# Block sums of A21 and A22, and one transfer of squares, put elsewhere in the written order of a factorization-machine kernel

## The chip, the cores and the metric

The kernel runs on one core of one Trainium2 chip. The metric is device time in microseconds (us); the time of a version is the median of several executions. Besides these, one execution is recorded by the hardware profiler; all lines of profiles in this document are of such an execution. PE is TensorE's matmul row and PEld its weight loads, DVE is VectorE, ACT is ScalarE, POOL is GpSimd, SP is SyncE, and a q behind a name is that engine's sequencer, which issues transfers and waits.

## The reference

Input x has 1024 rows of 512 features. There are 64 embeddings, each a 512 x 512 matrix, one linear layer of 512 x 512 and a bias:

```python
out_lin = x @ lin_w.T + lin_b
xv = jnp.einsum('bf,efm->bem', x, weight)
zp = jnp.einsum('bf,efm->bem', jnp.square(x), jnp.square(weight))
interaction = 0.5 * jnp.sum(jnp.square(xv) - zp, axis=1)
return out_lin + interaction
```

All is float32. The second product is linear in the squared weights, so the kernel sums these over the embeddings first (`w2_sum`) and multiplies by the squares of x once, at the end. What remains is 64 products of x with an embedding, squared and summed.

## The kernel before

**Tiling.** x is taken as 2 x 2 blocks A11, A12, A21, A22 (`"1"`, `"2"`, A21 apart, `"4"`), each again as 2 x 2 quarters. The embeddings are worked through in 16 groups of four ("quads", q = 0 to 15). In a quad the product is done with seven products in place of eight, on two levels: seven units i (in the order 1, 2, 6, 7, 5, 3, 4), each with seven products o (1, 5, 6, 2, 7, 3, 4), for two halves j of the rows. For this, sums and differences of blocks of x (`outer_x`, `inner_x`; made once) and of weights (`outer_t`, `inner_t`; on GpSimd in each quad) are needed. A product ends in a PSUM bank x, v or y; ScalarE copies x to y (line 481), VectorE and ScalarE read the banks and add them to earlier parts of the unit chain in the buffers `z` (lines 450 to 473). Two adds of unit 5 (`rest`, line 478) are GpSimd's. ScalarE squares the finished z in place (line 503), and GpSimd issues transfers that add z to the running sum `acc` (`gather`, line 512).

**Weights.** Four buffers hold a quad's weights (`WB[kk][v]`, 1 MB each), loaded by SP (line 364). ScalarE squares them (`w_squares`, line 521), two instructions to half a quad's pair, into the one buffer `w2_sb` (`w_sb` in the profile). GpSimd issues a transfer that adds this buffer to `w2_sum` (`w_sum` in the profile, line 528). The next squares can be written only when that transfer has landed. The very first squares go straight to `w2_sum`.

**Order.** Each engine works in the order of a list. `Stream.at(t, fn)` enters a piece of work under a time t of an abstract clock, and `run` carries the pieces out sorted by t; so t only decides the order on each engine, and waits between engines do the rest. One quad is 98 of these units, one product two. An engine does not go on past a piece that waits.

**The beginning.** Before quad 0 the linear layer is done. `lin` (line 215) makes the rows of A11's products; then come two units in the same seven-product form, unit 0 for A12 (`lin_unit(0, ...)`, line 347) and unit 1 for A21 and A22 (`lin_unit(1, ...)`, line 348). Products are line 272. VectorE reads a bank of unit 0 in `lin_add` (line 315), at 0.25 behind its product: banks v, y, x, v, y, y, at -20.25, -19.25, -18.25, -17.25, -16.25 and -13.65. Product "4" of unit 0 adds to bank y after the read of "7". Unit 1 needs the sums 5, 6, 7, 3 of the quarters of A21 and A22, which `a21_a22_sums` makes on VectorE (line 252, kk = 0 for A21 and 1 for A22, in the order 5, 5, 6, 6, 7, 7, 3, 3). The list at line 595 gives them their times; where fewer times stand than there are pieces, the rest follow the last one at 0.1 each. In the same list stand the x sums for unit 3, six instructions of GpSimd (`outer_x("3")`, line 174, and `inner_x("3")`, lines 181 to 184).

**GpSimd in the first quad.** Around the piece that moves, its order before is: t6 of unit 7 (line 399, 34.5), the six x sums for unit 3 (36.9 to 37.4), the gather into acc (38.8), t4 of unit 7 (39.7), the transfer into `w2_sum` (42), then tp of unit 5 (43.1).

Of the kernel before, what the change touches and what calls it, by code (L numbers as in the profile page):

```python
# [28 lines left out]
def kernel(  # L29
# [31 lines left out]
    nc = tc.nc  # L61
# [45 lines left out]
    def xsl(i, o):  # L107
        return xs[:, SLOT[i], SLOT[o], :]
# [37 lines left out]
    def quarter(r, kk, n):  # L146

        w = slice(0, 3) if n is None else n
        for i, rk in BLOCK.items():
            if rk == (r, kk):  # L150
                return a21[i] if n == 3 else xs[:, SLOT[i], w, :]
        return A21[:, w, :]

    def outer_x(i, eng=nc.vector):
        if i in BLOCK:
            return []

        def put(n):
            w = slice(0, 3) if n is None else n

            def of(o):
                return a21[o] if n == 3 else xs[:, SLOT[o], w, :]

            def src(r, kk):
                return quarter(r, kk, n)

            if i == "5":
                eng.tensor_add(of(i), src(1, 0), src(1, 1))
            elif i == "6":
                eng.tensor_sub(of(i), of("5"), src(0, 0))  # L170
            elif i == "7":
                eng.tensor_sub(of(i), src(0, 0), src(1, 0))
            else:
                eng.tensor_sub(of(i), src(0, 1), of("6"))

        return [lambda: put(None), lambda: put(3)]

    def inner_x(i, eng=nc.vector, which="5673"):
        add, sub = eng.tensor_add, eng.tensor_sub
        fns = {  # L180
            "5": lambda: add(xsl(i, "5"), a21[i], xsl(i, "4")),
            "6": lambda: sub(xsl(i, "6"), xsl(i, "5"), xsl(i, "1")),
            "7": lambda: sub(xsl(i, "7"), xsl(i, "1"), a21[i]),
            "3": lambda: sub(xsl(i, "3"), xsl(i, "2"), xsl(i, "6")),
        }
        return [fns[o] for o in which]
# [45 lines left out]
    def lin_x(kk, o, r=1):  # L232
        if r == 0:
            return xsl("2", o)
        if kk == 1:
            return xsl("4", o)
        return A21[:, SLOT[o]] if o in "124" else A21_SUMS[:, "5673".index(o)]


    def a21_a22_sums():  # L240
        def put(kk, o):
            def of(o):
                return lin_x(kk, o)

            raw = a21["4"] if kk else A21[:, 3]
            fn, a, b = {
                "5": lambda: (nc.vector.tensor_add, raw, of("4")),
                "6": lambda: (nc.vector.tensor_sub, of("5"), of("1")),
                "7": lambda: (nc.vector.tensor_sub, of("1"), raw),
                "3": lambda: (nc.vector.tensor_sub, of("2"), of("6")),  # L250
            }[o]()
            fn(of(o), a, b)

        return [
            lambda o=o, kk=kk: put(kk, o)
            for o in "5673"
            for kk in range(2)
        ]
# [257 lines left out]
    def w_squares(t, q, v, u):  # L516
        first = q == v == u == 0

        def sq(kk):
            o = (w2_sum if first else w2_sb)[:, ts(kk, 2)]  # L520
            nc.scalar.activation(o, WB[kk][v][:, u], AF.Square)  # L521

        for kk in range(2):
            st.at(t + 0.1 * kk, lambda kk=kk: sq(kk))
        if not first:
            st.at(
                t + (3.2 if t < 0 else 5),
                lambda: nc.gpsimd.dma_start(w2_sum, w2_sb, accum_op=ALU.add),
            )

# [10 lines left out]
    for q in range(NQ):  # L541
# [29 lines left out]
        for k, n, r, times in (  # L571
# [5 lines left out]
            for j in range(2):  # L577
                t = g0 + 14 * k + 7 * j + 14.6
# [8 lines left out]
        for n, t in enumerate(w_times):  # L587
            w_squares(g0 + t, q, n // 2, n % 2)
# [6 lines left out]
    for sums, *times in (  # L595
        (inner_x("1"), -29),
        (inner_x("2"), -22),
        (a21_a22_sums(), -21, -19, -18, -16.9, -15.9),
        (outer_x("5") + outer_x("6") + inner_x("6"), -13.5),
        (outer_x("7"), -6),  # L600
        (inner_x("7", which="75"), -5.4),
        (inner_x("7", nc.gpsimd, "6"), -5),
        (inner_x("7", nc.gpsimd, "3"), -4.7),
        (inner_x("5", nc.gpsimd), 27.2),
        (outer_x("3", nc.gpsimd) + inner_x("3", nc.gpsimd), 36.9),
    ):
        for n, fn in enumerate(sums):
            k = min(n, len(times) - 1)
            st.at(times[k] + 0.1 * (n - k), fn)
# [233 lines left out]
```

## Time and profile before

| | us |
|---|---|
| median of 3 runs | 1411.3 (1410.71 to 1411.66) |
| profiled execution | 1412.15 |
| its span, first to last instruction | 1410.3 |
| PE busy | 1402.1 |
| DVE busy | 867.2 |
| ACT busy | 621.3 |
| POOL busy | 1252.2 |
| mean rate of the DMA engines | 194 GB/s |

A row of a timeline gives the start, the duration, the engine, the line and operation, what is written and read, the shape and the count; in brackets, the engine's idle time before it and what ended that. In the chain of waits the columns are start, duration and what the time went to; "issue" is time in which the engine waited for nothing that the profile shows. A transfer that GpSimd or SP issues shows as a short instruction; the data move later.

### The profile page before, as it was taken

How to read it: one execution, taken by the hardware profiler on the slowest of the kernel's cores; microseconds unless marked ns; L12 is line 12 of the kernel's file. 1: busy time of each engine (PE TensorE's matmuls, PEld its weight loads, DVE VectorE, ACT ScalarE, POOL GpSimd, SP SyncE). 2: the span in 40 equal slices, each digit the busy share in tenths (PEclk: the TensorE clock that was granted, in tenths of full speed). 3: DMA queues.
4: the chain of work that ended last, by engine and by line, in shares of the span. 5: the costliest groups of instructions: out<-in, count | busy, mean ns of one | idle time of the engine just before them, and what ended most of it. 6: DMA issues, size and time to landing. Idle time of an engine off the chain costs nothing.

```text
span 1410.3 us, 11201 instructions
## 1 busy us (share of the span) xinstructions
PE 1402.1 (99%) x3352; PEld 637.6 (45%) x3352; DVE 867.2 (61%) x1270; ACT 621.3 (44%) x826; POOL 1252.2 (89%) x815
## 2 busy tenths in 40 slices
PE   9999999999999999999999999999999999999999
PEld 6444444444444444444444444444444444444446
DVE  6555666656566565666656566565656656566565
ACT  2435353443534434353443534444353453435443
POOL 3999899998999989899898988989898898989984
PEclk9999999999999999999999999999999999999999
DMA  5199898898989899898999989989898999989975
GB/s 216 30 222 212 179 221 178 206 212 205 193 170 233 179 212 210 190 212 168 218 196 220 197 171 228 182 201 214 193 206 173 223 187 218 203 175 225 181 165 134
DMA packets 58108, 273.63 MB, mean 194 GB/s; under 512 B 5440, under 2 KB 8000, under 8 KB 41792
## 3 DMA queue, kind: packets, MB, share of 16 engines
q0 software_dynamic: 36432, 198.20, 71.7%
q1 hardware_dynamic: 21328, 74.19, 15.1%
q10 hardware_dynamic: 288, 0.52, 0.1%
q8 instruction: 27, 0.44, 0.1%
q14 instruction: 33, 0.27, 0.1%
HBM read 72.61 MB, written 2.10 MB: 53 GB/s over the span
## 4 chain that ended last, share of the span: by engine, by line
PE 92%; POOL 4%; DMA 2%; issue 1%; DVE 0%; ACT 0%; POOLq 0%; ACTq 0%; DVEq 0%
PE y L427 39%; PE v L427 26%; PE x L427 26%; DMA acc<-z 1%; DMA w_sum<-w_sb 1%; POOL tp L397 1%; PE lin L215 1%; POOL t L386 0%; POOL t L401 0%; PE y_lin L272 0%; POOL t L399 0%; POOL acc L512 0%; POOL z L478 0%; POOL w L386 0%; DMA t<-lin_wT 0%
## 5 line engine op out<-in xcount | busy, mean ns | idle before, releaser
L427 PE MATMUL y<-t,xs 128*128 128x512 f32 x896 | 421.3, 592 | 0.0
L481 ACT COPY y<-x 128x512 f32<-128x512 f32 x224 | 127.7, 570 | 607.5 <-PE x L427 607.4
L473 DVE TENSOR_TENSOR z<-y,s 128x512 f32<-128x512 f32 x192 | 132.9, 692 | 249.5 <-PE y L427 249.5
L427 PEld LDWEIGHTS y<-t,xs 128*128 128x128 f32 x896 | 170.2, 190 | 214.3 <-issue 212.1
L503 ACT ACTIVATE z<-z 128x1024 f32<-128x1024 f32 x256 | 260.1, 1054 | 11.7 <-POOL z L478 9.2
L427 PE MATMUL x<-w,xs 128*128 128x512 f32 x512 | 248.4, 592 | 0.0
L427 PE MATMUL y<-tp,xs 128*128 128x512 f32 x448 | 229.4, 594 | 2.3 <-ACT s L450 2.3
L427 PE MATMUL v<-tp,xs 128*128 128x512 f32 x448 | 229.6, 594 | 0.0
L512 POOL DMA_DIRECT2D acc<-z x190 | 213.2, 1152 | 14.4 <-DMA acc<-z 9.2
L397 POOL TENSOR_TENSOR tp<-w 128x1024 f32<-128x1024 f32 x64 | 175.0, 2734 | 26.6 <-PE y L427 22.0
L427 PE MATMUL x<-t,xs 128*128 128x512 f32 x384 | 188.3, 592 | 0.0
L478 POOL TENSOR_TENSOR z<-z,s 128x1024 f32<-128x1024 f32 x64 | 149.6, 2355 | 41.8 <-DVE s L473 41.8
L473 DVE TENSOR_TENSOR z<-v,s 128x512 f32<-128x512 f32 x192 | 132.9, 692 | 73.4 <-PE v L427 71.6
L464 DVE TENSOR_TENSOR z<-y,z 128x512 f32<-128x512 f32 x192 | 132.5, 690 | 57.2 <-PE y L427 57.2
L386 POOL TENSOR_TENSOR t<-w,t 128x1024 f32<-128x1024 f32 x64 | 164.2, 2727 | 0.0
L464 DVE TENSOR_TENSOR z<-x,z 128x512 f32<-128x512 f32 x192 | 132.3, 689 | 36.5 <-PE x L427 35.0
L427 PEld LDWEIGHTS x<-w,xs 128*128 128x128 f32 x512 | 97.3, 190 | 122.0 <-issue 120.8
L397 POOL TENSOR_TENSOR tp<-t 128x1024 f32<-128x1024 f32 x48 | 130.1, 2711 | 19.4 <-PE y L427 19.2
L427 PEld LDWEIGHTS y<-tp,xs 128*128 128x128 f32 x448 | 85.0, 190 | 109.4 <-issue 106.0
L427 PEld LDWEIGHTS v<-tp,xs 128*128 128x128 f32 x448 | 85.4, 191 | 107.5 <-issue 103.9
L427 PE MATMUL v<-w,xs 128*128 128x512 f32 x256 | 130.7, 592 | 0.0
L521 ACT ACTIVATE w_sb<-w 128x1024 f32<-128x1024 f32 x126 | 125.9, 1050 | 6.3 <-DMA w_sum<-w_sb 4.7
(117 smaller groups left out, 1456.4 us busy)
## 6 DMA issues: line engine op xcount, KB each, us to landing
w<-weight SPq DMA_DIRECT2D x64, 1024.0 KB, 13.1
acc<-z POOLq DMA_DIRECT2D x128, 512.0 KB, 8.3
w_sum<-w_sb POOLq DMA_DIRECT2D x63, 1024.0 KB, 9.5
acc<-z POOLq DMA_DIRECT2D x62, 1024.0 KB, 8.4
w<-x SPq DMA_DIRECT2D x2, 1024.0 KB, 8.0
out<-z SPq DMA_DIRECT2D x7, 256.0 KB, 2.3
xs<-x SPq DMA_DIRECT2D x2, 384.0 KB, 7.4
t<-lin_wT ACTq DMA_DIRECT2D x2, 256.0 KB, 4.3
```

The lines of the kernel that those rows point to most:

```text
L215: nc.tensor.matmul(LIN[n], quarter(0, 0, (0, 1, 3, 2)[2 * s + l])[:, ts(j, P)], lw_sb[:, l, :], start=(l == 0), stop=(l == 1),)
L386: nc.gpsimd.tensor_sub(OUTER[i][:, u], a[:, u], b[:, u])
L397: nc.gpsimd.tensor_sub(t, b[:, 1], b[:, :, 0])
L427: nc.tensor.matmul(d[bank], xsl(i, o)[:, ts(j, P)], operand_b(q, i, o), start=start, stop=True, skip_group_check=True,)
L464: nc.vector.tensor_add(zblk(q, dst, j, b), d[bank], zblk(q, addend, j, b))
L473: nc.vector.tensor_add(s if both else zblk(q, dst, j, b), d[bank], s)
L478: nc.gpsimd.tensor_add(place(q, n)[:, 1, j], place(q, src)[:, 1, j], d["s"])
L481: st.at(t0 + 0.5, lambda: nc.scalar.copy(d["y"], d["x"]))
L503: lambda u=u: nc.scalar.activation(z[:, u, j], z[:, u, j], AF.Square),
L512: nc.gpsimd.dma_start(o, z, accum_op=ALU.add)
L521: nc.scalar.activation(o, WB[kk][v][:, u], AF.Square)
```

## The change

Three numbers of the order change. The sum "5" of A22 goes from -19 to -20.9, so it follows "5" of A21 at once, ahead of the reads of banks v and y at -20.25 and -19.25. The six sums 6, 7 and 3 go to -15.9 and after, so "6" of A21 and of A22, which stood at -18 and -16.9 among the reads, now follow the read of bank y at -16.25. For quad 0, v = 1, u = 0, the transfer of squares into `w2_sum` goes from 5 to 1.5 behind the squares, from 42 to 38.5 in GpSimd's order. The x sums for unit 3 go from 36.9 to 38.9. GpSimd's order becomes: t6 of unit 7, the transfer into `w2_sum`, the gather into acc, the six x sums, t4 of unit 7, tp of unit 5.

```diff
         if not first:
             st.at(
-                t + (3.2 if t < 0 else 5),
+                t + (3.2 if t < 0 else 1.5 if q == 0 and v == 1 and u == 0 else 5),
                 lambda: nc.gpsimd.dma_start(w2_sum, w2_sb, accum_op=ALU.add),
             )
...
-        (a21_a22_sums(), -21, -19, -18, -16.9, -15.9),
+        (a21_a22_sums(), -21, -20.9, -15.9),
...
-        (outer_x("3", nc.gpsimd) + inner_x("3", nc.gpsimd), 36.9),
+        (outer_x("3", nc.gpsimd) + inner_x("3", nc.gpsimd), 38.9),
```

## The prediction

> **What bounds the kernel now.** The page first. TensorE is busy nearly all the time, so what counts is where it isn't, or where it runs slowly.
>
> ```profile
> PE 1402.1 (99%) x3352; PEld 637.6 (45%) x3352; DVE 867.2 (61%) x1270; ACT 621.3 (44%) x826; POOL 1252.2 (89%) x815
> ```
>
> Then the busy time by stretches (stretch, length; busy us of PE, PEld, DVE, ACT, POOL; granted clock; DMA share; GB/s):
>
> ```profile
> 0.00:35.00 35.00, 32.49 (x111) 21.57 (x112) 21.64 (x36) 10.28 (x16) 13.15 (x16) 1.00 0.59 218
> 70.00:92.00 22.00, 19.69 (x43) 8.41 (x42) 10.61 (x16) 5.17 (x8) 20.31 (x15) 0.92 0.89 178
> 92.00:110.00 18.00, 18.00 (x43) 7.96 (x43) 13.41 (x21) 10.10 (x12) 16.94 (x12) 1.00 1.00 264
> 175.00:1345.00 1170.00, 1170.00 (x2728) 517.95 (x2727) 724.17 (x1058) 524.28 (x695) 1066.17 (x686) 1.00 0.91 200
> ```
>
> From 175 to 1345 us TensorE has no gap. It loses time at the start, in 70 to 92 (where alone the clock is under 1.00), and a little at the end. The chain of waits, in order of time, goes through both early places:
>
> ```profile
> 15.67 0.22 DVE xs L252
> 15.89 2.17 issue
> ...
> 73.04 10.88 DMA w_sum<-w_sb
> ...
> 87.02 1.65 PE y L427 x2
> ```
>
> One DVE sum with 2.17 us in it that no wait explains; and a transfer of squares that ScalarE, and behind it TensorE, waits for. Both are what the diff moves. The timeline of the first place, all engines:
>
> ```profile
> 15.51 2.35 POOL L397 TENSOR_TENSOR tp<-w 128x1024 f32<-128x1024 f32 x1 [3.31 <-DMA w<-weight]
> ...
> 15.67 2.47 DVE L252 TENSOR_TENSOR xs<-z,xs 128x256 f32<-128x256 f32 x1
> ...
> 20.76 1.10 PE L272 MATMUL y_lin<-z,xs 128*128 128x256 f32 x4 [1.49 <-DVE acc L315]
> ```
>
> The sum of A22 ("5" of kk=1) at 15.67 meets a GpSimd operation that began 0.16 us before; it lasts 2.47 us where its like takes 0.41, and ends just after GpSimd does. Three bank reads queue behind it on VectorE, and TensorE's last product of unit 0 waits for the third. The second place:
>
> ```profile
> 71.22 0.85 POOL L512 DMA_DIRECT2D acc<-z  x1
> ...
> 73.04 1.17 POOL L528 DMA_DIRECT2D w_sum<-w_sb  x1
> ...
> 84.00 2.00 ACT L521 ACTIVATE w_sb<-w 128x1024 f32<-128x1024 f32 x2 [4.69 <-DMA w_sum<-w_sb]
> ...
> 104.16 2.00 ACT L521 ACTIVATE w_sb<-w 128x1024 f32<-128x1024 f32 x2 [1.58 <-DMA w<-weight]
> ```
>
> The first of the two ScalarE lines is the wait for the transfer; the second, for a load of weights, matters for what is late next.
>
> **What the Trainium skill says.** "SBUF — State Buffer", Who interferes with whom: a VectorE instruction with two SBUF inputs contends with a GpSimd instruction that reads SBUF, the later one blocks until the first ends; one with at most one SBUF input doesn't. The trace agrees: the sum's 2.47 us, against bank reads of 0.69 us under running GpSimd work. "TensorE: Matmul & The Clock Gate", What's actually happening: after an idle window of some 3.4 us, free-running, the array runs at half clock until it has been busy for one. The trace agrees in kind, with only 2.3 us idle: after 87.02 the steps between products are 1.44, 1.71 and 1.22 us instead of 0.86. "DMA: Bandwidth & Descriptors", Issuing engines are not separate DMA queues: SP's and GpSimd's transfers interleave on the same 16 engines. The trace agrees: in 92 to 110 their share is 1.00.
>
> **The change part by part.** The sum is made against the span, 1410.3 us (the profiled execution took 1412.15); the median shown is 1411.3. I take the same difference off each.
>
> *Block sums (VectorE).* Eight sums before, eight after, none added. "5" of kk=1 goes from behind two bank reads to right behind "5" of kk=0. It then starts at 13.42 (0.34 after its neighbour, the pitch of such sums at 20.53, 20.86, 21.20) and ends by 13.83, inside VectorE's wait of 0.63 us before 14.12: cost nothing. If that cover were gone it would cost 0.34. Its new wait is on block A22: the semaphores put its last landing at 12.88, so 0.54 to spare, and 0.29 more until it holds up the read at 14.12. GpSimd is idle from 12.20 to 15.51, so no collision. The other six sums go behind the read at 16.52 + 1.14 = 17.66 (a read follows the start of its products by 1.14: 12.98 to 14.12). They begin at about 18.3, after GpSimd's operation ended (17.86) and before its next (30.31). TensorE needs "6" three products later, at about 21.7; it is ready by 19.1. Six of 0.34 end near 20.4, when the last read of unit 0 is due (20.24): 0.15 us, covered by VectorE's later wait of 1.08 at 28.87.
> TensorE's gain: products before the gap start at 17.38 and 18.24, after it at 20.76, 21.70, 22.56. With 0.86 a step 21.70 would be 19.96: **1.74 us**. GpSimd's restart at 30.31 waits for a VectorE sum that itself follows TensorE, so it moves 1.74 too.
>
> *The transfer of squares (GpSimd).* No operation is added. In GpSimd's order the issue of w_sum (73.04) and of one gather into acc (71.22) come ahead of the six x sums for "3" (65.80 to 71.27, 5.4 us); the product's t4 stays behind them. Each issue takes 0.60 of GpSimd's time (71.22 to 71.82), so the x sums end 1.2 us later, 20 us before their unit at about 94; everything from t4 on keeps its place. The new wait: the squares of that transfer end at 65.09, GpSimd arrives at 65.84, 0.75 to spare. Behind that wait would stand the gather, the x sums and all later GpSimd operands.
> w_sum is now issued at 65.84 - 1.74 = 64.1. The first such transfer, alone, took 8.2 us (48.49 to 56.72 by the semaphores), this one 10.88 behind the gather. It lands between 72.3 and 75.0; ScalarE wants its buffer at 79.31 - 1.74 = 77.6. The 4.69 us wait goes. TensorE gains 87.02 - (82.83 + 2 x 0.86) = 2.47 of idle time, and of the three slow steps 4.37 - 3 x 0.86 = 1.80: **4.27 us**. Both parts together: 6.0.
>
> *Where the stall goes.* GpSimd gains only 1.74 there. The rests at 92.44 waited 1.89 for VectorE; now GpSimd arrives at 88.81, late by 2.4 against TensorE's 6.0. Its tp for "4" ends at 101.9, while TensorE's use of it (107.70) moves to 101.7: 0.2 given back, at most 5.8 left. More comes from the weights of the second quad. SP issues them at 84.82 behind GpSimd's outer "4", so at 83.1. ScalarE already waits for the second load at 104.16 (its last landing is 104.05), then squares (1.91), squares again (0.97) and copies y (0.57): 107.66, and TensorE uses that y at 109.42. So 1.76 to spare: the total gain is at most what the load comes earlier, plus 1.76.
> How much earlier? The DMA engines are full from 72 to 106. The gather issued at 81.54 had to wait for w_sum until 83.92; now it starts when issued, at about 79.8 + 1.4 = 81.2, 2.7 us earlier, and the loads behind it. Against it: the gathers of 97.04 and 103.08 come 3.6 to 4.5 us earlier and share with the load. Bounds: 2.7 if they don't matter, 1.74 (its issue alone) if they do. I take 2.3, as only their lead over the load, one or two us, counts. Gain 2.3 + 1.76 = **4.1** (3.5 to 4.5). Afterwards TensorE has no gap to the end: GpSimd waits for it or for VectorE some 5 us a quad (41.2 and 41.8 us in 16), so it makes up its lag, and the tail's chain starts from TensorE at 1357.6. Forecast 1410.3 - 4.1 = 1406.2 of span, 1407.2 median.
>
> **The rivals.**
> A, likeliest (0.57): as above, gain 3.3 to 4.9.
> B (0.15): the load comes early enough, or ScalarE's copy has more room; only the 0.2 of tp is lost: 5.8, 1405.5. For it: its first engines finish at 100.6, the last alone at 104.05. Against: the same spread in later quads.
> C (0.15): the new gap on TensorE (6.0 - 4.1 = 1.9) trips its clock again and costs up to 1.8 more: gain about 2.3, 1409.0. For it: 2.3 us of idling did so at 87. Against: the gap of 1.49 at 19.27 did not.
> D (0.05): the sum gains nothing, because A22 arrives after 15: second part alone, limited by the load, about 2.5, 1408.8.
> E, slower (0.08): the two gathers, each about 2.5 us of full DMA at 200 GB/s, get wholly ahead of the load's last engines. It lands 5 - 2.7 = 2.3 later than before; with 1.76 to spare 0.5 is lost, and the clock's price of 1.8 to 3 comes on top: 2.3 to 3.5 slower, 1414. It decides from a landing 1.76 us later than today's 104.05. Against it: one of them is already before that landing today.
>
> **How the numbers follow.** A difference under 0.2% (2.8 us) can't be told from none here. A and B are faster, and a fifth of C: 0.75. The rest of C and D: same, 0.17. Slower: 0.08. From B's gain of 5.8 (and a little for the runs' spread) to the weak end of C, 1.3: 1405.4 to 1410.0, which leaves out E and edges.
>
> **What would show it.** After: a sum L252 of about 0.41 at 13.4, no 2.47; no TensorE wait on VectorE near 19; w_sum issued near 64, no ScalarE wait on it; clock 1.00 in 70 to 90. Then a ScalarE wait on weights grown from 1.58 to some 5 us near 97 to 102, and a TensorE gap of 1 to 2 us just before 105. Wrong if TensorE gets no gap there (B), if slow steps follow it (C), or if new gaps come in later quads, where I count none.

## The result and the profile after

The changed kernel takes 1407.41 us (median of 16 runs, 1406.9 to 1408.36), against 1410.82 us (1409.65 to 1411.66) for the kernel before beside it: a ratio of 0.9977, 95% interval 0.997 to 0.9985. That is 0.23% faster, clear of no change, and inside the forecast's range; the forecast was 1407.2. The profiled span is 1406.4 us (forecast 1406.2).

The page of the kernel after, busy time of each engine:

```profile
PE 1401.1 (100%) x3352; PEld 637.8 (45%) x3352; DVE 863.9 (61%) x1270; ACT 621.5 (44%) x826; POOL 1252.6 (89%) x815
```

Its busy time by the same stretches as before (stretch, length; busy us of PE, PEld, DVE, ACT, POOL; granted clock; DMA share; GB/s):

```profile
0.00:35.00 35.00, 34.15 (x114) 22.51 (x115) 20.32 (x36) 11.23 (x17) 14.21 (x16) 1.00 0.58 218
70.00:92.00 22.00, 22.00 (x53) 9.79 (x52) 13.54 (x21) 7.40 (x11) 21.77 (x16) 1.00 0.74 149
92.00:110.00 18.00, 16.76 (x40) 7.01 (x39) 11.83 (x18) 8.66 (x11) 17.18 (x12) 1.00 1.05 276
175.00:1345.00 1170.00, 1170.00 (x2727) 518.40 (x2726) 721.87 (x1057) 526.60 (x697) 1066.37 (x687) 1.00 0.91 199
```

The gap and the slow clock in 70 to 92 are gone. In 92 to 110, where TensorE had no gap before, it now lacks 1.24 us. From 175 to 1345 TensorE has no gap, as before. The chain of waits after, in order of time, passes through the first place without leaving TensorE, and leaves it at a new one:

```profile
18.04 1.73 PE x_lin L272 x8
19.77 0.86 PE y_lin L272 x4
...
84.09 17.82 DMA w<-weight
...
105.59 1.96 PE y L427 x4
```

VectorE's timeline after, at the moved sum:

```profile
13.09 0.41 DVE L252 TENSOR_TENSOR xs<-z,xs 128x256 f32<-128x256 f32 x1
14.62 0.69 DVE L315 SCALAR_TENSOR_TENSOR s_lin<-v_lin,acc 128x512 f32<-128x512 f32 x1 [1.12 <-PE v_lin L272]
```

The sum that took 2.47 us takes 0.41, inside a wait. ScalarE's timeline after, at the new place, and then TensorE's:

```profile
102.01 2.00 ACT L521 ACTIVATE w_sb<-w 128x1024 f32<-128x1024 f32 x2 [4.93 <-DMA w<-weight]
103.92 1.04 ACT L503 ACTIVATE z<-z 128x1024 f32<-128x1024 f32 x1
104.87 0.58 ACT L481 COPY y<-x 128x512 f32<-128x512 f32 x1
```

```profile
102.77 1.13 PE L427 MATMUL v<-tp,xs 128*128 128x512 f32 x2 [0.41 <-POOL tp L397]
103.73 1.02 PE L427 MATMUL v<-w,xs 128*128 128x512 f32 x2
105.59 1.96 PE L427 MATMUL y<-t,xs 128*128 128x512 f32 x4 [0.84 <-ACT y L481]
```

ScalarE waits 4.93 us for quad 1's second load (it landed at 101.91) instead of 1.58. TensorE loses time twice, first for GpSimd's tp of unit 4, then for the copy of y that stands behind ScalarE's squares. Counted in steps of 0.86 us from the product group at 100.49, the one at 107.38 is 1.7 us late.

### The profile page after: what moved, and what is told of

It is laid out like the page before. It is cut to its first block, busy times and chain, and to the rows that moved or that the text cites. A ratio compares the mean times of both kernels' runs of the same rounds, so it can differ in the third digit from the quotient of the medians.

```text
span 1406.4 us, 11202 instructions
## 1 busy us (share of the span) xinstructions
PE 1401.1 (100%) x3352; PEld 637.8 (45%) x3352; DVE 863.9 (61%) x1270; ACT 621.5 (44%) x826; POOL 1252.6 (89%) x815
## 4 chain that ended last, share of the span: by engine, by line
PE 95%; DMA 2%; POOL 2%; issue 0%; ACT 0%; DVE 0%; POOLq 0%; ACTq 0%; DVEq 0%
PE y L427 40%; PE x L427 27%; PE v L427 26%; DMA w<-weight 1%; DMA acc<-z 1%; PE lin L215 1%; PE y_lin L272 1%; PE x_lin L272 0%; PE v_lin L272 0%; POOL z L478 0%; POOL acc L512 0%; DMA t<-lin_wT 0%; POOL w_sb L660 0%; POOL tp L397 0%; POOL w L640 0%
## 5 line engine op out<-in xcount | busy, mean ns | idle before, releaser
L452 DVE TENSOR_TENSOR s<-v,z 128x512 f32<-128x512 f32 x160 | 110.5, 690 | 30.5 <-PE v L427 29.2
```

Of the source, the lines that this page charges most:

```text
L452: nc.vector.tensor_add(o, d[bank], zblk(q, addend, j, b))
```

## Experiments

Medians of the first four runs are against 1411.15 us for the kernel before beside them, of the next three against 1411.08, of the last three against 1410.97.

**The block sums alone.**

```diff
-        (a21_a22_sums(), -21, -19, -18, -16.9, -15.9),
+        (a21_a22_sums(), -21, -20.9, -15.9),
```

> The block sums moved, the transfer and the x sums left as before. My theory (a VectorE sum met a running GpSimd operation and held up three bank reads): the 2.47 us sum becomes 0.41, TensorE's wait on VectorE near 20 us is gone, all later work comes 1.7 us earlier, ScalarE still waits about 4.7 us for the transfer of squares and TensorE runs slowly behind it. Span 1408.6, 1.7 us below before. Rival (what is won early is lost again at the transfer or at the weights of quad 1): span within 0.5 us of before.

Measured 1409.09 us, ratio 0.9988 (0.9982 to 0.9995): 2.1 us faster. In the profile the linear product groups go 18.02, 18.89, 19.75, where before 18.24 was followed by 20.76 and 21.70: 1.73 us, as worked out. The bank reads at 15.63 and 16.50 run under GpSimd's operation (15.12 to 17.49) and take their usual 0.69. ScalarE still waits 4.74 us for the transfer and TensorE 2.36 us behind it. But no slow steps follow that wait here, and the span is 1406.6, 2 us below what I expected; the clock is taken up below.

**The transfer and the x sums alone.**

```diff
-                t + (3.2 if t < 0 else 5),
+                t + (3.2 if t < 0 else 1.5 if q == 0 and v == 1 and u == 0 else 5),
...
-        (outer_x("3", nc.gpsimd) + inner_x("3", nc.gpsimd), 36.9),
+        (outer_x("3", nc.gpsimd) + inner_x("3", nc.gpsimd), 38.9),
```

> The transfer of squares ahead of the x sums, the block sums left as before. My theory: the ScalarE wait on the transfer and the slow TensorE stretch go (4.3 us), but the second weight load of quad 1 is issued when it was, and lands only about 1 us earlier since the DMA engines have less ahead of it; ScalarE then waits some 4 us for it and TensorE gets a gap of about 1.5 us before 109. Gain 1.0 + 1.8 = 2.8, span 1407.5. Rival (the two stalls are independent and the load doesn't limit): gain 4.3, span 1406.0. If the two parts simply add up, this and the sums alone make the whole change's 3.9.

Measured 1408.39 us, ratio 0.9983 (0.9976 to 0.999): 2.8 us faster. ScalarE has no wait on the transfer, waits 4.61 us for the weights from then on, and TensorE waits 0.45 us for tp at 103.36 and 0.47 us for the copy of y at 105.82. The two parts alone give 2.1 and 2.8 us; together they give 3.4. They don't add up. With the transfer alone, quad 1's second load already holds TensorE up. With the sums alone hardly any spare time is left there: ScalarE's copy of y ends at 105.59, and TensorE uses it at 105.82. Both gains also hold a part of the same clock, which is counted below, at the kernel before once more.

**Only the "5" of A22 moved.**

```diff
-        (a21_a22_sums(), -21, -19, -18, -16.9, -15.9),
+        (a21_a22_sums(), -21, -20.9, -18, -16.9, -15.9),
```

> Of the block sums only the 5 of A22 goes ahead of the reads; both 6 stay among the reads. My theory (the collision with GpSimd's operation of 15.5 to 17.9 is the cause, whichever sum it hits): now the 6 of A21, due at about 16.6, is the one that lasts 1.5 us or more, the reads behind it are late, TensorE still waits about 1.3 us near 20. Gain 0.2 to 0.5, span 1410. Rival (the 5 of A22 waited for its data, or is slow by itself): the stall is gone, gain 1.7 as with all sums moved.

Measured 1410.3 us, ratio 0.9994 (0.9986 to 1.0002): 0.85 us faster, not told from none by its interval. The profile, GpSimd's line and then VectorE's:

```profile
14.75 2.36 POOL L397 TENSOR_TENSOR tp<-w 128x1024 f32<-128x1024 f32 x1 [2.70 <-DMA w<-weight]
```

```profile
16.59 0.80 DVE L252 TENSOR_TENSOR z<-z 128x256 f32<-128x256 f32 x1
```

The sum that is now hit is the "6" of A21, as the theory said. It ends at 17.39, 0.28 us after GpSimd's operation. In the kernel before the long sum ended at 18.14, also 0.28 after GpSimd (17.86). With the transfer alone it was 17.46 against 17.18:

```profile
15.26 2.20 DVE L252 TENSOR_TENSOR xs<-z,xs 128x256 f32<-128x256 f32 x1
```

Three sums of different length, each ending 0.28 us behind GpSimd: they waited for it, not for data. What I got wrong is the price. The sum that is hit here starts later, at 16.59, and GpSimd's operation, released by the first load of weights, started at 14.75, against 15.51 in the kernel before. So the sum loses only 0.4 us, and TensorE didn't wait in this execution. The median still lies 1.2 us above that of all sums moved. Part of that is the clock, which is taken up below: the mean granted clock of an execution is under 1.000 in 8 of the 13 here and in 5 of the 21 there, and among those at 1.000 the medians are 1409.35 and 1408.93, only 0.4 us apart. That the rest comes from a later start of GpSimd's operation is not shown; no such execution of this kernel was profiled.

**The x sums kept first.**

```diff
-        (outer_x("3", nc.gpsimd) + inner_x("3", nc.gpsimd), 38.9),
+        (outer_x("3", nc.gpsimd) + inner_x("3", nc.gpsimd), 36.9),
```

> The whole change, but the six x sums keep their place ahead of the transfer of squares and the gather. The transfer is then issued at about 70 instead of 64.6 us and lands at about 77 to 78, when ScalarE wants its buffer (78.0): a wait of 0 to 0.5 us. My theory (the whole gain is set by when the second load of quad 1 lands): the gather behind the transfer ends near 82 instead of 76.6 and holds the next gather and the loads up by 1 us, so the load lands about 1 us later, the gap of TensorE before 106 grows by about 1, and the span is 1407.4, 1 us above the whole change. Rival (only the wait on the transfer counts): span as with the whole change, 1406.4, within 0.3.

Measured 1409.67 us, ratio 0.9993 (0.9986 to 0.9999): only 1.5 us faster than before, some 2 us slower than the whole change. The direction was right, and so was the hold on the next gather, expected near 82. Its price and its way to TensorE were not. ScalarE doesn't wait for the transfer (issued at 69.55). GpSimd's line, and TensorE's, in this run:

```profile
82.52 0.88 POOL L512 DMA_DIRECT2D acc<-z  x1 [2.59 <-DMA acc<-z]
```

```profile
104.98 1.12 PE L427 MATMUL v<-tp,xs 128*128 128x512 f32 x2 [2.02 <-POOL tp L397]
```

The next gather adds into the same half of acc as the one issued at 70.14, so GpSimd may not issue it until that one has landed, at 82.23. That holds up everything behind it on GpSimd: the loads' release (issued at 85.81, not 83.60), the rests, tp of unit 4. TensorE waits 0.80 us at 95.83 for VectorE, which had waited for the first of the rests, and then 2.0 us for tp. The load, at 103.26, is 1.35 later too, but it no longer decides. So the x sums' move to behind the gather carries weight, which the prediction had counted at nothing.

**ScalarE's squares behind the copy of y.**

```diff
-            w_times = (-19.2, 14.8, 37, 56.6)
+            w_times = (-13.4 if q == 1 else -19.2, 14.8, 37, 56.6)
```

> The whole change, and ScalarE's first squares of quad 1 (which wait for the load that lands near 102) stand behind the copy of y that TensorE needs, not ahead of it. Nothing is loaded earlier. My theory (TensorE's second gap, of 1.1 us before 106, is ScalarE waiting for that load ahead of the copy): that gap goes, the first (0.6 us, for GpSimd's tp of unit 4) stays, span 1405.3, 1.1 below the whole change. Rival (that gap is GpSimd's: the t6 of unit 4 is late anyway): span as with the whole change, 1406.4.

Measured 1407.13 us, ratio 0.9973 (0.9962 to 0.9984). The gap before 106 is gone: after the wait of 0.42 us for tp at 101.90 TensorE runs on to 113. There a new one comes, 0.39 us for the tp of quad 1's unit 1 at 114.57, and one more step late behind it. GpSimd now waits 1.25 us at 108.06 for a load with the squares' transfer and that tp still queued behind. So the gap was ScalarE's, as said, but what it cost came back behind it, and the time can't be told from that of the whole change (1407.0 in the last comparison).

**Loads earlier.** Outer and inner x sums go behind GpSimd's outer "4".

```diff
-        (outer_x("3", nc.gpsimd) + inner_x("3", nc.gpsimd), 38.9),
+        (outer_x("3", nc.gpsimd), 52.3),
+        (inner_x("3", nc.gpsimd), 53.5),
```

> The whole change, but GpSimd makes the x sums of unit 3 behind its outer 4 of quad 0 instead of ahead of t4: so SP issues quad 1's loads some 2.8 us earlier, all GpSimd work from the rests on stays. My theory: the second load lands near 99, ScalarE's squares end near 101 and the copy is in time; the second gap goes, the first stays, span 1405.3 as with the squares behind the copy. Rival (the loads land no earlier because the DMA engines are full): span 1406.4, the wait of ScalarE on the weights still near 4.9 us.

One part of the computation is changed by this: the quarter that these sums pass through lies in a buffer of z that unit 7 fills meanwhile, so unit 3's sums come from other data. The operations and their sizes are the same. Measured 1407.21 us, ratio 0.9974 (0.9964 to 0.9984). The second load lands at 94.73 instead of 101.91, ScalarE no longer waits for it, and TensorE has no gap between 85 and 1395. That answers the rival: the DMA engines could deliver earlier. But unit 7's write waits for the sums in the shared buffer, VectorE 3.50 us for line 174, and TensorE behind it:

```profile
78.75 1.12 PE L427 MATMUL y<-tp,xs 128*128 128x512 f32 x2 [1.28 <-DVE s L452]
```

So this says where the limit lies, and not what lifting it is worth.

**Loads earlier, and tp of unit 4 ahead of a gather.**

```diff
-            ("4", 81, 82.1, 84.1),
+            ("4", 81, 82.1, 84.1) if q else ("4", 79.9, 79.95, 84.1),
```

> As the run with earlier loads, and in quad 0 GpSimd makes tp and t6 of unit 4 ahead of the gather that stood before them. My theory (after the load, tp is the last thing that costs TensorE time here): no gap of TensorE between 85 and 1395, 1.7 us below the whole change, span 1404.7. Rival (with both covers restored something else is late, such as the gather that is now issued 4 us later and a buffer that waits for it): a new gap in quad 1, span 1405.3 or more.

On top of the last edit, with the same changed data. Measured 1407.27 us, ratio 0.9975 (0.9965 to 0.9985), TensorE's 1.30 us wait at 78.46 again its only one there. The wait hides what tp would have shown; inconclusive.

**The kernel before once more**, unchanged.

> The kernel before once more, for its profile. My theory now: TensorE's 2.3 us of waiting near 84 is in every execution, but the slow steps behind it (1.8 us) only in some, as the runs with that wait left in show none: here they may be missing, and the span is then about 1408.5; with them it is 1410.3. Rival (they always follow this wait in the kernel before): 1410.3 with three steps of 1.2 to 1.7 us.

Span 1409.6, with the slow steps. Why they are there and not behind the same wait in two other runs shows when the trace's record of the clock is laid over the wait. In both profiles of the kernel before this record has 81.92 us at full clock, then 3.413 us at half: 24 stretches of the same length, then one. So I cut the time into such stretches. The kernel before of the first profile (columns as above; the clock stands behind POOL):

```profile
84.07:87.48 3.41, 1.10 (x3) 0.30 (x2) 1.11 (x2) 3.38 (x5) 3.33 (x3) 1.00 1.05 197
87.48:90.89 3.41, 3.41 (x5) 1.33 (x4) 0.69 (x1) 0.48 (x1) 3.07 (x3) 0.50 0.98 216
```

And the run with the block sums alone, in stretches of the same length from the start of its own record of the clock:

```profile
80.26:83.68 3.42, 2.50 (x6) 0.76 (x4) 1.98 (x3) 1.58 (x2) 3.42 (x3) 1.00 0.91 182
83.68:87.09 3.41, 1.97 (x5) 1.01 (x6) 0.69 (x1) 1.88 (x4) 3.33 (x4) 1.00 0.99 160
87.09:90.50 3.41, 3.41 (x10) 1.50 (x9) 1.48 (x3) 1.17 (x2) 3.21 (x3) 1.00 0.91 211
```

In the first the whole wait of 2.31 us lies in one stretch, and the next runs at half clock. In the second a wait as long falls across a border, 0.9 and 1.4 us, and nothing follows. In the second profile of the kernel before 2.1 us lie in one stretch, and half clock follows; with the "5" alone moved it is 1.2 and 1.0, and none follows. The largest share of a stretch that TensorE lacked without half clock behind it, in all thirteen profiles from the start of the clock's record up to 1395 us, is 1.78 us, in the run with tp of unit 4 alone, below:

```profile
102.83:106.24 3.41, 1.63 (x5) 0.70 (x5) 1.06 (x3) 3.41 (x5) 2.80 (x5) 1.00 1.05 239
```

That fits the free-running window that the Trainium skill describes ("TensorE: Matmul & The Clock Gate", What's actually happening) better than my reading of it did: not the length of a wait decides, but how much of it falls into one window. The page puts half clock behind an idle window; here a window that was idle for 2.1 of its 3.41 us was enough, and one idle for 1.8 us was not.

How often the kernel before pays this can be told from the mean clock recorded for each execution. One stretch at half clock takes about 0.0012 off that mean (half of 3.41 in 1410 us), so it reads 0.999; where in the execution the stretch lay is not recorded. Of 97 executions of the kernel before beside these runs, 59 read under 1.000, with a median of 1411.34 us, and 38 read 1.000, with 1410.00. With the sums alone it is 5 of 21. With the transfer alone it is none of 19, and with the whole change none of 24: where the long wait is gone, so is the low clock. With the x sums first, which left a wait of 2.0 us, it is 4 of 21.

**All that was late covered.** Added to the whole change: tp and t6 of unit 4 ahead of the gather, the squares behind the copy of y, and quad 1's first transfer and the tp and t6 of its unit 1 ahead of the GpSimd operation that waits for a load.

```diff
-            ("1", -6.4, -1.4, 2.1) if q else ("1", -16, -4.9, -4.8),
+            ("1", -9.93, -9.92, 2.1) if q == 1 else ("1", -6.4, -1.4, 2.1) if q else ("1", -16, -4.9, -4.8),
...
-            ("4", 81, 82.1, 84.1),
+            ("4", 81, 82.1, 84.1) if q else ("4", 79.9, 79.95, 84.1),
...
-            w_times = (-19.2, 14.8, 37, 56.6)
+            w_times = (-13.4 if q == 1 else -19.2, 14.8, 37, 56.6)
...
-                t + (3.2 if t < 0 else 1.5 if q == 0 and v == 1 and u == 0 else 5),
+                t + (3.2 if t < 0 else 1.5 if q == 0 and v == 1 and u == 0 else 3.45 if q == 1 and v == u == 0 else 5),
```

> The whole change with each later lateness that the runs so far showed covered: in quad 0 tp and t6 of unit 4 ahead of the gather; in quad 1 ScalarE's first squares behind the copy of y, their transfer and tp and t6 of unit 1 ahead of GpSimd's outer 5, which waits for a load. My theory (these are all that is late): no gap of TensorE from 33 to 1395, 1.7 us below the whole change run beside it. Rival (GpSimd has no more time to give here, so each cover uncovers the next operand): a gap of 0.5 us or more somewhere in 100 to 130, and the gain over the whole change is under 0.8 us.

Measured 1405.88 us, ratio to before 0.9965 (0.9953 to 0.9978), 1.1 us below the whole change beside it. The intervals of the two ratios overlap, but each of its five executions (1405.19 to 1406.41) is below each of the eight of the whole change (1406.57 to 1407.82). Its stretches:

```profile
92.00:110.00 18.00, 18.00 (x43) 7.98 (x42) 13.09 (x21) 10.53 (x12) 17.26 (x12) 1.00 1.02 264
110.00:175.00 65.00, 64.93 (x152) 28.61 (x151) 37.95 (x56) 27.09 (x38) 61.34 (x40) 1.00 0.95 198
```

TensorE's 1.24 us in 92 to 110 are back. What is left of lateness is 0.3 us near 138, where the tp of quad 1's unit 6 is now late. The gain is 1.1 us, not the 1.7 expected, so the rival has a part: a cover uncovers the next operand.

**tp of unit 4 alone.** The whole change with the edit of `("4", ...)` alone.

> The whole change with only tp and t6 of unit 4 in quad 0 moved ahead of the gather before them. My theory (the load of quad 1, through ScalarE's squares, sets the total): TensorE's first gap (0.6 us near 102) goes and the second, before 106, grows by as much; time as the whole change within 0.3 us. Rival (GpSimd's operands set the total): 0.6 us below the whole change.

Measured 1407.18 us, ratio 0.9975 (0.9966 to 0.9985), as the whole change beside it. TensorE's line:

```profile
104.85 1.95 PE L427 MATMUL y<-t,xs 128*128 128x512 f32 x4 [1.78 <-ACT y L481]
```

One wait where there were two. By the steps TensorE is 1.9 us late behind it, against 1.7 behind both in the first profile of the change: lifting tp alone gives nothing, the copy of y behind the load takes it over.

**The whole change once more.**

> The whole change once more, beside the two above, for comparison on one chip and for a second profile: gaps of about 0.6 and 1.1 us on TensorE near 102 and 105, the second load near 102, span within 0.6 us of 1406.4.

Measured 1407.0 us, ratio 0.9973 (0.9962 to 0.9983), span 1404.8. The wait for tp is there (0.45 us at 101.94). The second load lands at 100.21 here, not at 101.91, and by the steps the second gap costs 0.2 us instead of 1.1. Half of the load's 1.7 us is the opening, as TensorE starts quad 0 at 29.96 here and at 30.83 in the first profile. The rest is the load itself, so its landing differs between executions, and the gain with it.

## Why the prediction was right

**Block sums.** Right in each step: the sum at 13.09 (forecast 13.42), 0.41 us, all hidden; the read of the third bank at 18.08 (17.66, with the opening itself 0.5 us later here), no wait of TensorE near 19, the last read at 20.70; 1.73 us by the steps of the run with them alone (forecast 1.74). That the collision and not late data made the sum long is shown by the three ends 0.28 us behind GpSimd, and by the bank reads that took 0.69 us under the same operation.

**The transfer.** Issued at 64.56 (forecast 64.1), landed at 71.59 (72.3 to 75.0), no ScalarE wait, clock 1.00. Incomplete by what I left out: that the gather's place counts. I priced the x sums' delay, 1.2 us that nobody waits for, but not the wait that their place behind the gather avoids. Kept first, they make GpSimd wait 2.59 us for a gather into the same acc, and cost 2 us in the median.

**The 4.27 us.** Its 1.80 us of slow steps were counted as if every execution had them. The step that failed is "the three slow steps": they are a matter of where the wait falls. Two profiles of the kernel before have them, two runs with the same wait don't, and by the recorded clocks 59 of 97 executions of the kernel before have them. So the second part alone is worth 2.5 to 4.3 us of TensorE's time, before the load limits it. The forecast came from an execution that had them. In the last comparison the gain is 4.4 us against the executions with a clock under 1.000 and 3.1 against the others.

**Where the stall goes.** Right in the first profile of the change, and the core of the forecast: 6.0 us won, and given back down to what the second load of quad 1 allows. Its landing was forecast at 104.05 - 2.3 = 101.75 and was 101.91; ScalarE's wait of "some 5 us" was 4.93; the gap of 1.9 us was 1.7. That it came so close is luck in part, since in the second profile the load landed at 100.21. There tp of unit 4 cost TensorE 0.7 us and the copy behind the load only 0.2, so the load is not the limit in every execution. The squares behind the copy, tp alone, and the two parts alone show each link: load, ScalarE's squares, copy of y, TensorE. They don't show that the load alone sets the time, because with the squares moved the time stayed and GpSimd's next tp was late; only with all of it covered did the time fall. Mis-sized was tp of unit 4: 0.2 us forecast, about 0.6 measured. It took 3.22 us behind the gather's issue instead of 2.64. In the first profile this cost nothing more, as the copy came later still. A small slip: the spare time of 1.76 us starts from a copy that ends at 107.66, but by the lines it ends at 107.61.

**The size.** By the medians the gain is 3.4 us in the first comparison and 4.0 in the last, of 4.1 forecast; by the spans of the first profiles it is 3.9. Case C's slow clock did not follow the new gap: at most 1.24 us of it lay in one stretch, and no recorded execution of the change reads a clock under 1.000. Case A stood.

## What to carry to other kernels

When two stalls in a row are removed, don't add them up: follow the transfer or operand that was on time only because of the stalls, and take the gain up to its spare time. A price read from one profile holds for executions like that one: the slow clock behind a wait was in some executions of the same kernel and not in others. Moving one issue ahead on an in-order queue moves its neighbours too; look at which later transfer adds into the same buffer and so waits for the one that was moved. And where a late operand and a late copy follow each other, lifting one may show nothing until the other is lifted as well, as here.

## What the runs showed of the hardware that was not expected

A TensorE wait of 2.2 to 2.4 us was followed by 3.41 us at half clock when 2.1 or 2.3 us of it lay in one 3.41 us stretch of the clock's record, and by none when it was split into at most 1.4 us; the most that lay in one stretch without half clock behind it was 1.78 us.

GpSimd's first tp, released by the first load of weights, started between 14.64 and 15.51 us in the thirteen profiles. A VectorE sum with two inputs in SBUF that met it ended 0.28 us behind it, whether it lasted 0.80, 2.20, 2.47 or 2.54 us.

GpSimd's tp of unit 4 took 2.64 us right behind a gather's issue in the kernel before, and 3.22 in the same place after the change. With that gather moved behind it, it took 2.52 to 2.95 us in three runs. What makes the difference was not tested.
